# Where VectorE sums a small gate network inside a matmul kernel: part of it one unit earlier, the rest one operation a slot

## The chip, the cores and the metric

One core of a Trainium2 chip runs the whole program. The metric is the device time of one execution in microseconds (us). The kernel before takes 2253.77 us (median of three runs, 2252.57 to 2255.48). Engines are named as in the profile: PE (TensorE), DVE (VectorE), ACT (ScalarE), POOL (GpSimd), SP (the queue from which nearly all DMAs are issued).

## The reference, cut to what matters

`x` is 2 x 2048 x 512, fp32. Layer 0 puts each batch row `b` through three experts (hidden width 2048): two shared ones and one that a label selects. A gate per row, made from token 0 alone, weighs them. Layer 1 multiplies by a selected 512 x 512 matrix. Both layers are residual.

```
eo, s0, s1 = dense(x, wi[label], wo[label]), dense(x, swi[0], swo[0]), dense(x, swi[1], swo[1])
gate_in = concat([eo[:, 0], s0[:, 0], s1[:, 0]])             # 1536 numbers per row
w = softmax(relu(gate_in @ g1) @ g2)                         # g1: 1536 x 512, g2: 512 x 3
x = x + eo * w[0] + s0 * w[1] + s1 * w[2]
x = x + x @ W[cat] + b[cat]
```

## The kernel before, in words

The rows are cut into four blocks of 1024 tokens. The work is a list of twelve **units** (`units`, L109): units 0 to 3 are shared expert 0 on the four blocks, 4 to 7 shared expert 1, 8 and 9 the selected expert of row 0, 10 and 11 that of row 1. A unit is an up-projection (`up`, L743) and a down-projection (`down`, L882), each done by a two-level fast matrix product with 7 x 7 small products.

**Slots.** The order of everything is written out by hand. `up` has 7 stages (`i` in the order 1, 6, 2, 5, 7, 4, 3), each of 14 slots (`SEQ_UP`, L410, numbered s = 0 to 13). A slot issues two 128 x 256 matmuls, and the profile keeps two records of each, so a slot is 4 records and a stage 56. `down` has 49 slots (`SLOTS_DN`), numbered 0 to 48 here, of 8 records each.

**Seeds.** The products of a stage add up in PSUM banks, and what is in a bank is read out between two products that go into it, plus an older partial sum ("seed" below). In `up`: at s = 0, 1 product x1 is read into the z bank (L815, or ACT L813 in the stages 1 and 5); at s = 4, 5 x6 is read (L821); at s = 7, 8 x7 is read and a second sum is made (L821, L826); at s = 10, 11 L839; at s = 12, 13 L845. The next product into the same bank can't start before the read is done: x6 (s = 4, 5) waits for the reads of s = 0, 1; x7 (s = 7, 8) for those of s = 4, 5. `wide` (L776) and `make_tops` (L715) add DVE sums of 1024 columns, three of them at s = 11, 12, 13 of stage `i` = 5 and one at s = 1 of the next. In `down` the same reads are L947, L955, L957, L964, L966, with operand sums L733 to L740 and L904 and the block sums `y_sums` (L910).

**Background work.** `other_bg` is a list of generators; `step(other_bg)` (L871, L1022), at the end of every slot, advances the first one to its next `yield`. DVE, PE, ACT and SP each take their instructions in the order in which this program emits them, so what a generator emits stands behind that slot's seeds and ahead of the next slot's.

- `gate(b, 8)` (L1037) is appended at the end of units 8 and 10 and so runs in the first stages of units 9 and 11. It loads all of `g1` (3 MB, L1042) and a broadcast `g2` (L1044), waits 8 slots, then emits twelve multiply-adds into `hid` one a slot (L1052, L1054), three slots later a matmul `pg` over the partitions (L1059), relu `act` (L1062), three products `prod` (L1066), one reduction over 1536 columns (L1069), and the softmax (L1071 to L1081).
- `layer1(blk, 14)` (L1126) stands behind it, and also runs in unit 10 for the block of unit 9. It starts with `layer1_weights` (L1087): load W and a bias row, wait 14 slots, add the identity to W's diagonal (four 128 x 128 sums in one slot, L1101), then a matmul `pb` (L1104) and a copy (L1105). Then come 8 row tiles, 7 slots each: scaling on ACT (L1146), sums on POOL (L1151), four 512-column matmuls `po` (L1114), the result (L1122).
- `premix(blk, 10)` (L1169) is appended at the start of unit 11's `down`, behind `layer1` of unit 10's block: five loads of `acc` and `pm`, `layer1_weights` with a wait of 10 slots, then sixteen multiply-adds one a slot (L1192). At slot 47 whatever is left is emitted at once; `last_mix` (L1199) and the last 64 `po` records follow.

Weight blocks `w` come through 12 buffers, each fetched on SP 12 uses ahead (`used_w`, L631). The pool `io` has two buffers of 128 x 512 (tag `xn`).

Of the kernel before, what the change touches and what calls it, by code (L numbers as in the profile page):

```python
# [8 lines left out]
F32 = mybir.dt.float32  # L9
AF = mybir.ActivationFunctionType  # L10
ALU = mybir.AluOpType
AX = mybir.AxisListType
# [3 lines left out]
P = 128  # L16
# [3 lines left out]
ADD, SUB = ALU.add, ALU.subtract  # L20
# [16 lines left out]
def cond_resid_kernel(  # L37
# [22 lines left out]
    nc = tc.nc  # L60
    B, S, D = x.shape
# [681 lines left out]
    def up(n, xg, tops, y):  # L743
# [12 lines left out]
        for j, i in enumerate(I_UP(n)):  # L756
            mode, dst, src = plan[i]
            store = mode == "store"
            if dst not in O:
                O[dst] = qtile(n, f"h{dst}")  # L760
            if i == 5:
                O[12] = qtile(n, "h12")
            if n == 0 and i == 1:
                O[21] = qtile(n, "h21")
            half = lambda q, cc, d: blk_of(O[q], cc)[:, 2 * d : 2 * d + 2, :]
            bank, sn, seed = {}, {}, {}

            def relu(q, cc):
                v = blk_of(O[q], cc)
                nc.scalar.activation(v, v, AF.Relu)  # L770

            def wide(q, cc):


                o = blk_of(O[q], cc)
                nc.vector.tensor_tensor(o, blk_of(O[22], cc), blk_of(O[21], cc), ADD)  # L776
                if q == 22:
                    relu(22, cc)

            wides = {  # L780
                5: {11: (12, 11), 12: (12, 22), 13: (12, 21)},
                7: {1: (12, 12), 11: (22, 11), 13: (22, 22)},
                4: {1: (22, 21), 11: (22, 12)},
            }.get(i, {})
            done = False
            if i == (5 if n else 3):
                tg = make_tops(n, O, 1, 11, tops, y)
            top_at = {5: (2, 5), 3: (1, 11)}.get(i, ()) if n else (1, 3, 11, 13)
            for s, (bk, k, d) in enumerate(SEQ_UP):
                first = (bk, k) in (("x", 1), ("y", 5))  # L790
                if first:
                    bank[bk, d] = ps.tile(
                        [P, 2, TQ], F32, tag=bk, name=f"u{bk}_{n}_{i}_{d}"
                    )
                p = bank[bk, d]
                wt = w_tiles[n, 0, i, k]
                for g in range(2):
                    nc.tensor.matmul(  # L798
                        p[:, g, :],
                        lhsT=wt[:, 2 * d + g, :],  # L800
                        rhs=x_ops[n, i, k],
                        start=first and g == 0,
                        stop=True,
                        skip_group_check=True,
                    )
                if all(kk != k for _, kk, _ in SEQ_UP[s + 1 :]):
                    used_w()
                if k == 1:
                    z = bank["z", d] = ps.tile(
                        [P, 2, TQ], F32, tag="z", name=f"uz_{n}_{i}_{d}"  # L810
                    )
                    if store:
                        nc.scalar.activation(z, p, AF.Copy)  # L813
                    else:
                        nc.vector.tensor_tensor(z, p, half(src, 11, d), ADD)  # L815
                elif bk == "x" and k in SNAP:
                    t = snp.tile([P, 2, TQ], F32, tag="sn", name=f"us_{n}_{i}_{k}_{d}")
                    if store:
                        nc.scalar.activation(t, p, AF.Copy)  # L819
                    else:  # L820
                        nc.vector.tensor_tensor(  # L821
                            t, p, half(src, 12 if k == 6 else 22, d), ADD
                        )
                    sn[SNAP[k], d] = t
                    if k == 7:
                        nc.vector.tensor_tensor(  # L826
                            half(dst, 22, d), bank["y", d], t, ADD
                        )
                        if d == 1 and i in final:
                            relu(dst, 22)  # L830
                elif bk == "z":
                    nc.scalar.activation(  # L832
                        half(dst, 11, d), p, AF.Relu if i in final else AF.Copy
                    )
                elif k == 4:
                    if store:
                        nc.scalar.activation(half(dst, 21, d), p, AF.Copy)
                    else:
                        nc.vector.tensor_tensor(  # L839
                            half(dst, 21, d), p, half(src, 21, d), ADD  # L840
                        )
                    if d == 1 and i in final:
                        relu(dst, 21)
                elif k == 3:
                    nc.vector.tensor_tensor(half(dst, 12, d), p, sn["b", d], ADD)  # L845
                    if d == 1 and i in final:
                        relu(dst, 12)
                if s in wides:
                    wide(*wides[s])
                if n == 0 and i == 2:  # L850

                    for cc in {1: (11, 22), 2: (21,), 3: (12,)}.get(s, ()):
                        nc.scalar.activation(blk_of(O[21], cc), blk_of(O[11], cc), AF.Copy)
                if n == 0:
                    begin.outer({(2, 2): (7,), (6, 2): (3,)}.get((i, s), ()))
                    if (i, s) == (2, 2):
                        begin.second()
                    elif i in (5, 7) and s in (2, 5, 8, 11):
                        next(begin.ahead, None)
                    elif (i, s) == (4, 1):  # L860
                        for _ in begin.ahead:
                            pass
                if xg and j < 6 and not done and (
                    s >= 7 if i in (7, 4) else s % 2 == 0 or j == 0
                ):
                    done = advance(xg, 1)
                if s in top_at:
                    next(tg, None)
                prep_paced(RATE_UP[j])
                if n or j or s >= 7:  # L870
                    step(other_bg)  # L871
                if s == 4 and n not in MAKES and j + 2 < NP:
                    fetch_parts(n, I_UP(n)[j + 2])
            if xg and j < 6 and not done:
                advance(xg)
            if n in MAKES:
                keep_parts(n, i)
# [4 lines left out]
    def down(n, H, tops, y, prepare):  # L882
# [124 lines left out]
        for s, (i, name) in enumerate(SLOTS_DN):  # L1007
# [11 lines left out]
            prepare(s)  # L1019
            prep_paced(0.0)  # L1020
            prep_run(RUN_DN.get((i, name), 0))
            step(other_bg)  # L1022
        for _ in job:
            pass
# [7 lines left out]
        nc.sync.dma_start(out=ys[slot_y, blk], in_=yf)  # L1032

    gin = [const.tile([P, NX, DC], F32, name=f"gin_{b}") for b in range(B)]
    gates = {}

    def gate(b, lag):  # L1037


        g1t = [bigp.tile([P, 4, D], F32, tag=t, bufs=1, name=f"g1{t}_{b}") for t in ("raw", "o", "t")]  # L1040
        for j in range(NX):
            nc.sync.dma_start(out=g1t[j], in_=g1_v[:, j * DC : (j + 1) * DC, :])  # L1042
        g2b = bigp.tile([P, D, NX], F32, tag="s", bufs=1, name=f"g2b_{b}")
        nc.sync.dma_start(out=g2b, in_=g2.rearrange("(o d) n -> o d n", o=1).to_broadcast([P, D, NX]))  # L1044
        for _ in range(lag):
            yield
        hid = small.tile([P, D], F32, tag="hid", name=f"hid_{b}")
        for k in range(NX * DC):
            j, c = divmod(k, DC)
            col = gin[b][:, j, c : c + 1]  # L1050
            if k == 0:
                nc.vector.tensor_scalar(hid, g1t[j][:, c, :], col, None, ALU.mult)  # L1052
            else:
                nc.vector.scalar_tensor_tensor(hid, g1t[j][:, c, :], col, hid, ALU.mult, ADD)  # L1054
            yield
        for _ in range(3):
            yield
# [4 lines left out]
        nc.scalar.activation(act, pg, AF.Relu)  # L1062
        yield
        prod = bigp.tile([P, NX, D], F32, tag="o", bufs=1, name=f"prod_{b}")
        for j in range(NX):
            nc.vector.tensor_tensor(prod[:, j, :], act, g2b[:, :, j], ALU.mult)  # L1066
            yield
        logit = small.tile([P, NX], F32, tag="logit", name=f"logit_{b}")
        nc.vector.tensor_reduce(logit, prod, AX.X, ALU.add)  # L1069
        mx = small.tile([P, 1], F32, tag="mx", name=f"mx_{b}")  # L1070
        nc.vector.tensor_reduce(mx, logit, AX.X, ALU.max)  # L1071
        nc.vector.tensor_scalar(logit, logit, mx, None, ALU.subtract)
# [14 lines left out]
    def layer1_weights(blk, lag, also=None):  # L1087
# [7 lines left out]
        for k in range(lag):  # L1095
            yield
            if k == 5 and also:
                also()
        for c in range(DC):
            v = w1[:, c, c * P : (c + 1) * P]  # L1100
            nc.vector.tensor_tensor(v, v, ident, ADD)  # L1101
        yield
        pb = ps.tile([P, D], F32, tag="m", name=f"pb_{blk}")
        nc.tensor.matmul(pb, lhsT=ones[0:1, :], rhs=brow, start=True, stop=True)  # L1104
        nc.vector.tensor_copy(bias, pb)  # L1105
# [117 lines left out]
    with tc.manual_schedule():  # L1223
# [18 lines left out]
        for n, (e, blk) in enumerate(units):  # L1242
            if n == 0:
                for e0, k0 in [(e0, k0) for e0 in range(1, NE) for k0 in range(2)]:
                    preps[e0, k0] = Prep(e0, k0)
            tops = {}
            if n:
                y = yp.tile([P, DC, 4, TQ], F32, tag="y", name=f"y_{n}")
            H = up(n, xg, tops, y)
# [81 lines left out]
```

## Time and profile before

| | |
|---|---|
| three timed runs | 2252.57, 2253.77, 2255.48 us |
| the profiled execution, its own time | 2255.11 us |
| its span in the profile | 2253.3 us |
| granted TensorE clock in it | 0.994 |
| busy: PE / DVE / ACT / POOL | 2195.0 / 1637.5 / 544.4 / 722.4 us |
| HBM traffic | 421.80 MB read, 157.81 MB written |

How to read it: times in the views count from the start of the span, which is 1.8 us shorter than the execution's time. "Idle before" names what an engine waited for; only waits of an engine whose work ends last cost time. Units 8 to 11 begin near 1433, 1603, 1810 and 2010 us.

### The profile page before, as it was taken

To read this page: it belongs to the slowest core of one execution; us is meant where nothing else is said; L and a number is where in the kernel's file an instruction comes from. 1 tells how busy PE (TensorE), PEld (TensorE's weight loads), DVE (VectorE), ACT (ScalarE), POOL (GpSimd) and SP (SyncE) were. 2 spreads that over 40 slices of the span, in tenths; PEclk is the share of its full clock that TensorE was granted. 3 is DMA by queue.
4 is the path that set the end of the run, shared out by engine and by line. 5 is a ranking of instruction groups with operands and counts; after the bars stand their busy time and mean duration, and the time that the engine had idled before them with its cause. 6 is when DMAs were issued, how large, how long until landed. Compare 5 with 4: busy or idle time off the path is not lost.

```text
span 2253.3 us, 28548 instructions
## 1 busy us (share of the span) xinstructions
PE 2195.0 (97%) x9808; PEld 1851.5 (82%) x9808; DVE 1637.5 (73%) x2028; ACT 544.4 (24%) x937; POOL 722.4 (32%) x580
## 2 busy tenths in 40 slices
PE   8999998999999999999999999999999999999999
PEld 6787887888888888888888888888877877887786
DVE  7897778587688587587587587587676846767695
ACT  3221230331231231231131141131133133113310
POOL 5787522560850430340350340330033023002300
PEclk9999999999999999999999999999999999999999
DMA  9853996897997896896997896896896697579671
GB/s 339 317 170 108 352 311 210 292 312 253 301 327 217 289 326 179 301 310 205 300 311 216 273 333 215 274 335 183 294 293 185 185 318 227 153 250 321 207 276 56
DMA packets 484059, 581.55 MB, mean 258 GB/s; under 512 B 28360, under 2 KB 316104, under 8 KB 480716
## 3 DMA queue, kind: packets, MB, share of 16 engines
q1 hardware_dynamic: 480188, 572.90, 78.3%
q10 hardware_dynamic: 3728, 6.82, 0.9%
q8 instruction: 80, 1.31, 0.2%
q14 instruction: 63, 0.52, 0.1%
HBM read 421.80 MB, written 157.81 MB: 257 GB/s over the span
## 4 chain that ended last, share of the span: by engine, by line
PE 80%; DVE 9%; DMA 2%; POOL 2%; issue 1%; SPq 0%; ACT 0%; DVEq 0%; POOLq 0%; ACTq 0%
PE dx L933 23%; PE ux L798 20%; PE dy L933 12%; PE uy L798 9%; PE dz L933 6%; PE po L1114 5%; PE uz L798 5%; DVE h L904 1%; DMA w<-ws_s 1%; DVE h L776 1%; DMA g1raw<-in_L_cond_g_dram 1%; DVE y L910 1%; DVE hid L1054 1%; DVE us L821 1%; DVE h L845 1%
## 5 line engine op out<-in xcount | busy, mean ns | idle before, releaser
L798 PE MATMUL ux<-xs,w 128*128 128x256 f32 x1792 | 429.8, 381 | 11.0 <-DVE sm L1077 3.1
L933 PE MATMUL dx<-t,w 128*128 128x256 f32 x1680 | 399.2, 381 | 13.8 <-DVE ds L955 13.8
L798 PEld LDWEIGHTS ux<-xs,w 128*128 128x128 f32 x1792 | 337.5, 190 | 73.9 <-DVE us L821 9.6
L933 PEld LDWEIGHTS dx<-t,w 128*128 128x128 f32 x1680 | 319.2, 191 | 59.2 <-DVE ds L955 13.7
L1151 POOL TENSOR_TENSOR mix<-mix 128x512 f32<-128x512 f32 x72 | 102.3, 1421 | 523.9 <-DMA w<-ws_t 316.5
L821 DVE TENSOR_TENSOR us<-ux,h 128x512 f32<-128x512 f32 x240 | 162.7, 686 | 117.6 <-PE ux L798 117.2
L904 DVE TENSOR_TENSOR h<-h,h 128x1024 f32<-128x1024 f32 x192 | 241.1, 1271 | 0.0
L770 ACT ACTIVATE h<-h 128x1024 f32<-128x1024 f32 x156 | 164.5, 1056 | 240.2 <-DVE h L826 111.8
L798 PE MATMUL uy<-xs,w 128*128 128x256 f32 x896 | 214.4, 380 | 4.1 <-DVE h L845 3.9
L826 DVE TENSOR_TENSOR h<-uy,us 128x512 f32<-128x512 f32 x168 | 116.1, 692 | 112.3 <-ACT us L819 107.8
L798 PEld LDWEIGHTS uy<-xs,w 128*128 128x128 f32 x896 | 169.4, 190 | 34.3 <-DVE h L845 7.5
L832 ACT ACTIVATE h<-uz 128x512 f32<-128x512 f32 x168 | 99.5, 592 | 377.3 <-PE uz L798 350.5
L933 PE MATMUL dy<-h,w 128*128 128x256 f32 x672 | 160.4, 382 | 4.8 <-DVE y L957 4.8
L681 POOL TENSOR_TENSOR seen<-pulse 1x1 f32<-1x1 f32 x18 | 11.8, 656 | 474.7 <-DVE pulse L680 474.7
L798 PE MATMUL ux<-xi,w 128*128 128x256 f32 x640 | 154.1, 384 | 7.9 <-DVE us L821 2.8
L141 POOL TENSOR_TENSOR po<-pr 128x384 f32<-128x384 f32 x48 | 51.6, 1090 | 332.0 <-DMA w<-ws_s 127.4
L776 DVE TENSOR_TENSOR h<-h,h 128x1024 f32<-128x1024 f32 x96 | 146.1, 1522 | 7.0 <-ACT h L832 5.6
L845 DVE TENSOR_TENSOR h<-uy,us 128x512 f32<-128x512 f32 x168 | 113.0, 687 | 52.3 <-PE uy L798 50.1
L933 PEld LDWEIGHTS dy<-h,w 128*128 128x128 f32 x672 | 128.0, 191 | 23.8 <-issue 5.2
L933 PE MATMUL dz<-h,w 128*128 128x256 f32 x616 | 145.6, 379 | 0.1
L933 PE MATMUL dx<-h,w 128*128 128x256 f32 x616 | 145.5, 379 | 0.0
L798 PEld LDWEIGHTS ux<-xi,w 128*128 128x128 f32 x640 | 121.1, 191 | 29.7 <-issue 11.8
(155 smaller groups left out, 3332.7 us busy)
## 6 DMA issues: line engine op xcount, KB each, us to landing
w<-ws_t SPq DMA_DIRECT2D x352, 256.0 KB, 4.1
w<-ws_s SPq DMA_DIRECT2D x270, 256.0 KB, 4.3
w<-ws_o SPq DMA_DIRECT2D x264, 256.0 KB, 4.8
xs<-xs SPq DMA_DIRECT2D x56, 896.0 KB, 6.9
ws_s<-ps SPq DMA_DIRECT2D x24, 1024.0 KB, 7.6
ws_t<-pt SPq DMA_DIRECT2D x24, 1024.0 KB, 5.8
ys<-y SPq DMA_DIRECT2D x11, 2048.0 KB, 8.3
ws_o<-po SPq DMA_DIRECT2D x24, 768.0 KB, 7.6
```

Of the source, the lines that this page charges most:

```text
L141: eng.tensor_tensor(o, i0, i1, op)
L770: nc.scalar.activation(v, v, AF.Relu)
L776: nc.vector.tensor_tensor(o, blk_of(O[22], cc), blk_of(O[21], cc), ADD)
L798: nc.tensor.matmul(p[:, g, :], lhsT=wt[:, 2 * d + g, :], rhs=x_ops[n, i, k], start=first and g == 0, stop=True, skip_group_check=True,)
L821: nc.vector.tensor_tensor(t, p, half(src, 12 if k == 6 else 22, d), ADD)
L826: nc.vector.tensor_tensor(half(dst, 22, d), bank["y", d], t, ADD)
L832: nc.scalar.activation(half(dst, 11, d), p, AF.Relu if i in final else AF.Copy)
L845: nc.vector.tensor_tensor(half(dst, 12, d), p, sn["b", d], ADD)
L904: nc.vector.tensor_tensor(bl(o), bl(i0), bl(i1), SUB)
L933: nc.tensor.matmul(p, lhsT=wt[:, g, :], rhs=op[g], start=first and g == 0, stop=True, skip_group_check=True,)
L1114: nc.tensor.matmul(po[t], lhsT=mixed[c], rhs=l1[blk][0][:, c, :], start=(c == 0), stop=(c == DC - 1),)
L1151: nc.gpsimd.tensor_tensor(m[:, 3, :, :], m[:, 3, :, :], m[:, j, :, :], ADD)
```

## The change

`gate_shared(b)` is new. It is appended at the start of units 8 and 10 (`n in (2 * NB, 2 * NB + NBB)`), loads the eight 128 x 512 pieces of `g1` that belong to the shared experts one by one into the `xn` buffers, and emits the eight multiply-adds for them, five slots or more apart. `gate` keeps four multiply-adds and one load of 1 MB. A flag `quiet` is set in `up` at s = 0 to 3 and 11 to 13 and throughout `down`; `when_quiet` yields until it is set. The eight operations, the four that are left, the products, the reduction (cut into three of 512 columns) and the four diagonal sums each wait for such a slot and have one to themselves.

```
@@ up @@
             for s, (bk, k, d) in enumerate(SEQ_UP):
+                quiet[0] = s in (0, 1, 2, 3, 11, 12, 13)
@@ down @@
+            quiet[0] = True
             step(other_bg)
@@ new @@
+    def when_quiet():
+        while not quiet[0]:
+            yield
+    def gate_shared(b):
+        hid = hids[b] = small.tile([P, D], F32, tag="hid", name=f"hid_{b}")
+        t = {}
+        def fetch(k):
+            t[k] = iop.tile([P, D], F32, tag="xn", name=f"g1_{b}_{k}")
+            nc.sync.dma_start(out=t[k], in_=g1_v[:, k, :])
+        fetch(DC)
+        for k in range(DC, NX * DC):
+            if k + 1 < NX * DC:
+                fetch(k + 1)
+            for _ in range(4):
+                yield
+            yield from when_quiet()
+            j, c = divmod(k, DC)
+            col = gin[b][:, j, c : c + 1]
+            if k == DC:
+                nc.vector.tensor_scalar(hid, t[k], col, None, ALU.mult)
+            else:
+                nc.vector.scalar_tensor_tensor(hid, t[k], col, hid, ALU.mult, ADD)
+            yield
@@ gate @@
-        g1t = [bigp.tile([P, 4, D], F32, tag=t, bufs=1, name=f"g1{t}_{b}") for t in ("raw", "o", "t")]
-        for j in range(NX):
-            nc.sync.dma_start(out=g1t[j], in_=g1_v[:, j * DC : (j + 1) * DC, :])
+        g1t = bigp.tile([P, DC, D], F32, tag="raw", bufs=1, name=f"g1_{b}")
+        nc.sync.dma_start(out=g1t, in_=g1_v[:, :DC, :])
...
-        for k in range(NX * DC):
...
+        hid = hids[b]
+        for c in range(DC):
+            yield from when_quiet()
+            col = gin[b][:, 0, c : c + 1]
+            nc.vector.scalar_tensor_tensor(hid, g1t[:, c, :], col, hid, ALU.mult, ADD)
             yield
...
         for j in range(NX):
+            yield from when_quiet()
             nc.vector.tensor_tensor(prod[:, j, :], act, g2b[:, :, j], ALU.mult)
             yield
-        nc.vector.tensor_reduce(logit, prod, AX.X, ALU.add)
+            yield from when_quiet()
+            nc.vector.tensor_reduce(logit[:, j : j + 1], prod[:, j : j + 1, :], AX.X, ALU.add)
+            yield
@@ layer1_weights @@
         for c in range(DC):
+            yield from when_quiet()
             v = w1[:, c, c * P : (c + 1) * P]
             nc.vector.tensor_tensor(v, v, ident, ADD)
-        yield
+            yield
@@ main loop @@
+            if n in (2 * NB, 2 * NB + NBB):
+                other_bg.append((f"s{n}", gate_shared((n - 2 * NB) // NBB)))
```

More of the change, by code (lines that the diff above doesn't have):

```diff
@@ L1034, in cond_resid_kernel @@
     gin = [const.tile([P, NX, DC], F32, name=f"gin_{b}") for b in range(B)]
-    gates = {}
+    gates, hids = {}, {}
+    quiet = [True]
+    def when_quiet():
[21 more added lines that the diff above has]
+            yield
     def gate(b, lag):
-        g1t = [bigp.tile([P, 4, D], F32, tag=t, bufs=1, name=f"g1{t}_{b}") for t in ("raw", "o", "t")]
-        for j in range(NX):
-            nc.sync.dma_start(out=g1t[j], in_=g1_v[:, j * DC : (j + 1) * DC, :])
+        g1t = bigp.tile([P, DC, D], F32, tag="raw", bufs=1, name=f"g1_{b}")
+        nc.sync.dma_start(out=g1t, in_=g1_v[:, :DC, :])
         g2b = bigp.tile([P, D, NX], F32, tag="s", bufs=1, name=f"g2b_{b}")
@@ L1046, in gate @@
             yield
-        hid = small.tile([P, D], F32, tag="hid", name=f"hid_{b}")
-        for k in range(NX * DC):
[L1049 to L1054, printed above, removed]
+        hid = hids[b]
[3 more added lines that the diff above has]
+            nc.vector.scalar_tensor_tensor(hid, g1t[:, c, :], col, hid, ALU.mult, ADD)
             yield
@@ L1064, in gate @@
         prod = bigp.tile([P, NX, D], F32, tag="o", bufs=1, name=f"prod_{b}")
+        logit = small.tile([P, NX], F32, tag="logit", name=f"logit_{b}")
         for j in range(NX):
+            yield from when_quiet()
             nc.vector.tensor_tensor(prod[:, j, :], act, g2b[:, :, j], ALU.mult)
             yield
-        logit = small.tile([P, NX], F32, tag="logit", name=f"logit_{b}")
-        nc.vector.tensor_reduce(logit, prod, AX.X, ALU.add)
+            yield from when_quiet()
+            nc.vector.tensor_reduce(logit[:, j : j + 1], prod[:, j : j + 1, :], AX.X, ALU.add)
+            yield
         mx = small.tile([P, 1], F32, tag="mx", name=f"mx_{b}")
```

## The prediction, written before the changed kernel was run

> **What bounds the kernel now.** First the page: the busy times, then the chain that ended last.
>
> ```profile
> PE 2195.0 (97%) x9808; PEld 1851.5 (82%) x9808; DVE 1637.5 (73%) x2028; ACT 544.4 (24%) x937; POOL 722.4 (32%) x580
> ...
> PE 80%; DVE 9%; DMA 2%; POOL 2%; issue 1%; SPq 0%; ACT 0%; DVEq 0%; POOLq 0%; ACTq 0%
> ```
>
> PE sets the time, and the change takes no matmul away. It can only win back time in which PE stands still, so I looked for where that is. I took the distance between the first matmuls of successive stages in the timeline and subtracted the records in between, at 0.215 us for 256 columns and 0.429 us for 512 (a 56-record stage without a stall then takes 12.04 us). What is left, "loss", is 0.05 us for most stages. Up-projection of unit 8: 1.18 us in all. Unit 9: 0.05, 4.04, 1.94, 1.12, 0.43, 0.43, 0.43, together 8.45. Unit 10: 3.10. Unit 11: 0.05, 4.18, 1.95, 1.12 and three times 0.43, together 8.59, and its down-projection 4.26 (0.44, 1.36 and 2.28 in its third to fifth stages). 4 and 2 us stand exactly where the gate runs. The 0.43 are the price of two `po` tiles.
>
> Next, busy time by stretch: the two gates, and the same 25 us of unit 8.
>
> ```profile
> core 0: us, PE busy (x) PEld busy (x) DVE busy (x) ACT busy (x) POOL busy (x), PEclk, DMA share, GB/s
> 1615.00:1640.00 25.00, 21.03 (x88) 15.77 (x88) 23.64 (x39) 2.00 (x4) 0.00 (x0) 1.00 0.99 365
> 2022.00:2047.00 25.00, 20.89 (x88) 15.65 (x87) 23.69 (x39) 2.00 (x4) 0.00 (x0) 1.00 0.98 367
> 1445.00:1470.00 25.00, 25.00 (x117) 22.03 (x116) 16.93 (x25) 4.19 (x6) 13.89 (x12) 1.00 1.00 317
> ```
>
> In the gate DVE is full (23.6 of 25) and PE is not; in unit 8 it is the other way round. Then DVE's timeline in the first gate:
>
> ```profile
> 1615.12 0.49 DVE L1052 TENSOR_SCALAR hid<-g1raw,gin 128x512 f32<-128x512 f32 x1 [2.21 <-DMA g1raw<-in_L_cond_g_dram]
> 1615.64 2.33 DVE L1054 SCALAR_TENSOR_TENSOR hid<-g1raw,gin,hid 128x512 f32<-128x512 f32 x3
> 1617.88 0.68 DVE L845 TENSOR_TENSOR h<-uy,us 128x512 f32<-128x512 f32 x1
> 1618.48 0.74 DVE L1054 SCALAR_TENSOR_TENSOR hid<-g1o,gin,hid 128x512 f32<-128x512 f32 x1
> ...
> 1631.79 0.85 DVE L1066 TENSOR_TENSOR prod<-act,g2b 128x512 f32<-128x512 f32 x1
> ...
> 1635.90 1.74 DVE L1069 TENSOR_REDUCE logit<-prod 128x3 f32<-128x1536 f32 x1
> ```
>
> Every slot of 0.86 us holds a seed (next start 0.60 later) and a gate operation (0.66): 1.26 us of DVE. PE waits for the seeds (waits of PE's weight loads, 1613 to 1640):
>
> ```profile
> PEld ux L798 <- DVE sm L1077: 2.0, 1, 2.0
> PEld uy L798 <- DVE h L845: 2.0, 2, 1.4
> PEld ux L798 <- DVE us L821: 1.8, 2, 1.2
> PEld ux L798 <- DVE uz L815: 1.3, 3, 0.5
> ```
>
> "sm" is only what stood last in DVE's queue: the seed behind it was late because of the 1.74 us reduction.
>
> **The gate in units 9 and 11.** Eight of twelve multiply-adds leave. I followed slots against DVE's queue. With a wait of 8 slots, three of the four land at s = 11, 12, 13 of stage 1 and one at s = 0 of stage 2, beside the L845 seeds (0.60 each) and the z seeds. DVE work from s = 12 on: seed, 0.78, seed, 0.78, seed, 0.78, seed; the seed of s = 0 is read 3.4 us after the first, and x6 needs it 4.05 us after: no stall, and the seed of s = 1 fits too (4.7 against 4.9). `g1raw` landed 10.4 us after its issue with 2 MB more behind it; if the 1 MB takes as long, everything shifts by 0.85 us and stalls up to 0.8. I take 0.3. Stage 2 then costs 0.30 for the `pg` records plus 0.05 plus 0.3 = 0.65 instead of 4.04.
>
> The products and reductions fall on s = 11 to 13 of stage 2 and 0 to 2 of stage 3. A 512-column reduction is not in the trace. Two rows give it: 3 columns 0.156 us (L1071), 1536 columns 1.750, so 0.153 + 512 x 1.04 ns = 0.69, bounds 0.58 (a third) and 1.75. Queue: 0.60 + 0.77, 0.60 + 0.73, 0.60 + 0.77, 0.60 + 0.73, 0.60 + 0.77, 0.73, then the small ones (0.5): the z seed of s = 1 is done 0.2 us after x6 wants its bank, and the x6 seeds of s = 4, 5 start 1.5 us late, 0.7 to 0.9 us more than x7 allows, then 0.4. Stage 3: 1.7 instead of 1.94. Here the stall only changes its name.
>
> The cutting itself adds 2 x 0.15 = 0.3 us of DVE per gate, which is within that 1.7. [...]
>
> **W's diagonal.** Four sums of 0.284 us (start to start 0.22). Before, they came at s = 2 of stage 4, where ACT does the z seeds and DVE idles. With the later gate and `quiet` they come 12 slots later in all: s = 11, 12, 13 of stage 4 (`i` = 5, where three `wide` sums stand) and s = 0 of stage 5, then `pb` and its copy (0.60). In unit 8 the seeds of stage 5 are already a touch late there (0.39 loss). They get 0.45 and 0.66 us later; the two `pb` records (1.15 us on PE) come just before x6 and give that time back. Then the copy delays the x6 seeds and x7 waits 0.6. Stage 5: 0.3 (`pb`) + 0.6 + 0.2 = 1.1 instead of 0.43; stage 4: 0.05 instead of 1.12, since `pb`, `po` and mixing have left it. Stages 6 and 7: 0.43 each. Three `po` tiles move into the down-projection, whose slots are 1.72 us and whose loss is 0.05 with DVE at about 80%: nothing, at most 0.4.
>
> Unit 9: 0.05 + 0.65 + 1.7 + 0.05 + 1.1 + 0.86 = 4.4 instead of 8.45: **-4.05**. Unit 11: 4.4 instead of 8.59: **-4.2**. Bounds of each: -6.7 if stages 2, 3 and 5 lose nothing but their own records, -1 if stages 3 and 5 lose 2.5 us more.
>
> **Unit 8 gets eight multiply-adds** (0.75 us each, two a stage: s = 11 and 2), until s = 2 of stage 5. In stages 1 to 4 they meet idle DVE (16.93 of 25 above). The last stands behind the stage-5 `wide`, where DVE is 10.96 of 12 busy, and moves the x6 seeds by 0.7, which x7 feels in full. **+0.8**; bounds 0 (all hidden) and 8 x 0.75 = 6. POOL works in this unit and not in the gate. `wide` (L776) takes 1.21 to 2.35 us over the run, which I put down to POOL; 0.75 may then become 1.4 for some, which the upper bound holds. [...]
>
> SP gets eight 256 KB loads, and each waits for the multiply-add two before. Behind them stand the fetches of w. These land in 7.3 us in this stretch (median 4.1 over the run) and are issued 12 uses, about 20 us, ahead: 12 us of cover against waits of 1 to 2 us. If that cover went, PE would lose those waits, up to 8 x 1 us. A load is issued 12 us before its multiply-add, so DVE shouldn't wait; behind such a wait stand seeds, and PE waits for them.
>
> **Unit 10:** its multiply-adds fall into two up-stages and then slots 2 to 22 of the down-projection, with one every five slots of 1.72 us: 0, at most +1. Its diagonal goes from one slot to s = 0 to 3: the 0.76 us that PE waited behind it may go, but `po` moves by three slots: 0, bounds -0.8 and +0.8.
>
> **The last down-projection.** This is the part that the diff doesn't show. `layer1` ends 12 slots later in unit 11, so `premix` starts at slot 16 instead of 4, its diagonal at 26 to 29 instead of 14, its sixteen multiply-adds at 31 to 46 instead of 16 to 31. Before, DVE was full where they stood (busy time by stretch), and PE waited (timeline of PE and DVE):
>
> ```profile
> 2163.00:2197.00 34.00, 31.52 (x143) 26.48 (x142) 33.90 (x43) 3.81 (x10) 0.00 (x0) 1.00 0.65 219
> ```
>
> ```profile
> 2161.84 0.90 DVE L1101 TENSOR_TENSOR w<-w,ident 128x128 f32<-128x128 f32 x4 [1.71 <-DMA w<-in_L_cond_W_dram]
> ...
> 2182.96 1.99 PE L933 MATMUL dy<-h,w 128*128 128x256 f32 x8 [0.74 <-DVE y L957]
> ...
> 2191.94 1.99 PE L933 MATMUL dx<-t,w 128*128 128x256 f32 x8 [1.39 <-DVE ds L955]
> ```
>
> That loss (4.26 in all) goes, another comes. Counted from the start of slot 29, with start-to-start times 1.13 (L904, L733), 0.66 (L1192), 1.33 (a pair of L910) and 0.34 to 0.46 (seeds), DVE is never idle from slot 32 on: at slot 35 its work ends at 17.0 us while PE is at 13.2, at slot 38 at 26.3 against 18.4. `y` of slot 39 (L957) is done at 26.7, and y3 of slot 42, ready at 24.4, waits 2.4 us for it. ACT waits for `y_sums` at slot 36 and makes x7 0.8 late. After slot 42 DVE catches up, and the last `po` finds its operands. Loss 2.4 + 0.8 + 0.3 (`pb`) + 0.4 (others) = 3.9: **-0.4**. W landed 20.2 us after `premix` began; again so, it lands at the start of slot 29, and DVE has just enough to do after that. Each us later is one us more at slot 42. Bounds -3 (no stall) and +3.
>
> **Sum** against the profiled execution (span 2253.3, own time 2255.11): -4.05 - 4.2 + 0.8 + 0 - 0.4 = -7.8, so 2247.3. The median of the runs is 1.34 below that execution, which gives **2246.0**.
>
> **Rivals.**
> 1. *The gate's stall moves instead of going*: the z seeds of stage 3 and the crowd at `i` = 5 lose 2.5 us more in each gate. For it: DVE has 1.3 us per slot there still. Against: stage 2 (4 us) is relieved in any case. -7.8 + 5 = -2.8: 2251.
> 2. *Unit 8 pays it back*: all eight multiply-adds show, 6 instead of 0.8. For: DMA share 1.00 and POOL busy. Against: 8 us of idle DVE per 25. -2.6: 2251.
> 3. *The gate costs only its records*: -6.7, -6.85, +0.8, -0.4 = -13.1: 2240.7.
> 4. *Slower*: in the last down-projection W lands late, and `premix` stands wholly in the last 20 slots. The price is a us per us; with more than 7.8 us (W after 28 us instead of 20) the kernel is slower, and with 13 it takes 2259. For: 6 MB are loaded in one piece, ahead of it. Against: the same loads took 20.2 us at 367 GB/s, and nothing is added to them.
> 5. *It doesn't do what it says*: no; in the changed program's order on each engine the operations stand in the slots named above.
>
> **Chances.** Forecast 0.60 (2242.5 to 2249), rivals 1 and 2 0.15 and 0.07 (near 2251), 3 0.12, 4 0.06. A measurement of this kernel can tell about 0.2% (4.5 us) from no change: below 2249.3 is faster, 0.60 + 0.12; rivals 1 and 2 are the same, 0.22; slower 0.06. The range 2240 to 2252 leaves out rival 4 and the ends of 3 and 2, about 0.15.
>
> **What would show it.** Stage losses by the same count: unit 9 and 11 stage 2 under 1 us (right) or over 2 (wrong); stage 3 near 1.7; stage 5 near 1.1; unit 8's stage 5 near 1.1; a wait of "dy" for L957 of 2 to 3 us late in the last down-projection. A DVE wait of more than 1 us for W there, or for `g` tiles in unit 8, would make it wrong, as would a PE wait for w.

## The result, and the profile after

| | us |
|---|---|
| after, median of seven runs | 2263.89 (2260.02 to 2270.04) |
| before, median of seven runs beside them | 2253.77 (2252.57 to 2257.02) |
| ratio, 95% interval | 1.0045 [1.0035, 1.0056] |
| after's profiled execution, own time / span | 2269.35 / 2267.6 |

The forecast was 2246.0, 0.35% faster; the kernel is 0.45% slower. The page of after, its line of busy times and the engines of the chain that ended last:

```profile
PE 2196.7 (97%) x9808; PEld 1854.9 (82%) x9808; DVE 1651.3 (73%) x2032; ACT 544.5 (24%) x937; POOL 728.7 (32%) x580
...
PE 79%; DVE 8%; DMA 3%; POOL 3%; issue 1%; SPq 1%; ACT 0%; DVEq 0%; POOLq 0%; ACTq 0%
```

PE's work is the same, so again only the losses tell. Counted as in the prediction, in us (the last two columns are kernels described below; "sum" is over these units):

| | before | predicted | after | e1_act_queue | v2_shared_in_down |
|---|---|---|---|---|---|
| unit 8, up | 1.18 | 2.0 | **13.88** | 3.88 | 1.37 |
| unit 9, up | 8.45 | 4.4 | 4.43 | 4.81 | 3.60 |
| unit 9, down | 0.33 | 0.3 to 0.7 | **2.33** | 2.32 | 0.33 |
| unit 10, up | 3.10 | 3.1 | 0.73 | 0.73 | 0.73 |
| unit 11, up | 8.59 | 4.4 | 4.43 | 4.42 | 3.60 |
| unit 11, down | 4.26 | 3.9 | **9.82** | 9.82 | 3.68 |
| sum | 25.9 | 18.1 | 35.6 | 26.0 | 13.3 |

After minus before is 9.7 us, and the medians differ by 10.1: units 8 to 11 hold the whole result. In units 0 to 7, where nothing was changed, this one execution happens to be 4.4 us longer.

The gate's sum came out as forecast, though by errors that cancel (below). Busy time by stretch of after, some 11 us into units 9 and 11 as before, and the same 25 us of unit 8:

```profile
core 0: us, PE busy (x) PEld busy (x) DVE busy (x) ACT busy (x) POOL busy (x), PEclk, DMA share, GB/s
1449.00:1474.00 25.00, 22.81 (x106) 19.78 (x105) 17.35 (x25) 1.89 (x4) 12.75 (x11) 1.00 0.98 322
1495.00:1502.00 7.00, 5.39 (x12) 3.60 (x13) 6.84 (x8) 0.00 (x0) 6.92 (x5) 0.52 0.99 342
1632.00:1657.00 25.00, 24.48 (x110) 20.29 (x109) 22.04 (x38) 2.96 (x6) 0.00 (x0) 1.00 0.93 341
2035.00:2060.00 25.00, 24.47 (x110) 20.29 (x109) 22.02 (x38) 3.31 (x6) 0.00 (x0) 1.00 0.92 335
```

PE is busy 24.5 of 25 us in the gates instead of 21. But unit 8 has lost 2.2 us in the first row, and the second row has a granted clock of 0.52. What happened there is read from three engines. SP's queue, DVE and PE around 1480 to 1502 us of after:

```profile
1480.86 9.74 SPq L179 DMA_DIRECT2D pr<-in_L_cond_wo_dram  x8
1490.70 0.38 SPq L1052 DMA_DIRECT2D g<-in_L_cond_g_dram  x1
```

```profile
1486.23 1.22 DVE L776 TENSOR_TENSOR h<-h,h 128x1024 f32<-128x1024 f32 x1 [0.23 <-ACT h L833]
1495.16 0.79 DVE L1066 SCALAR_TENSOR_TENSOR hid<-g,gin,hid 128x512 f32<-128x512 f32 x1 [7.70 <-DMA g<-in_L_cond_g_dram]
1495.87 0.68 DVE L846 TENSOR_TENSOR h<-uy,us 128x512 f32<-128x512 f32 x1
```

```profile
1496.61 4.01 PE L799 MATMUL uy<-xs,w 128*128 128x256 f32 x8 [5.92 <-DVE h L846]
1500.48 2.76 PE L799 MATMUL ux<-xs,w 128*128 128x256 f32 x8
1503.08 1.03 PE L799 MATMUL uz<-xs,w 128*128 128x256 f32 x4
```

Eight loads of `pr` (raw weights for the background sums on POOL, L179) take SP 9.7 us to issue. One piece of `g1` stands behind them. DVE waits 7.7 us for it, a seed (L846) stands behind the multiply-add, and PE waits 5.9 us for the seed. Then PE's next records take 0.48 us each instead of 0.215: the granted clock is halved from 1495.2 to 1502.1. Part of that falls into the pause; the twelve records from 1496.61 on take 5.6 us instead of 2.6, so the half clock costs another 3.0 us. The same block of `pr` stood in before, and there unit 8 lost 1.18 us: nothing that DVE waits for in order stood behind it. (Before, SP's queue:)

```profile
1472.68 9.84 SPq L179 DMA_DIRECT2D pr<-in_L_cond_wo_dram  x8
```

### The profile page after: what moved, and what is told of

The parts are those of the page before. It is cut to its first block, busy times and chain, and to the rows that moved or that the text cites. A ratio compares the mean times of both kernels' runs of the same rounds, so it can differ in the third digit from the quotient of the medians.

```text
span 2267.6 us, 28578 instructions
## 1 busy us (share of the span) xinstructions
PE 2196.7 (97%) x9808; PEld 1854.9 (82%) x9808; DVE 1651.3 (73%) x2032; ACT 544.5 (24%) x937; POOL 728.7 (32%) x580
## 4 chain that ended last, share of the span: by engine, by line
PE 79%; DVE 8%; DMA 3%; POOL 3%; issue 1%; SPq 1%; ACT 0%; DVEq 0%; POOLq 0%; ACTq 0%
PE dx L934 22%; PE ux L799 20%; PE dy L934 11%; PE uy L799 9%; PE dz L934 6%; PE uz L799 5%; PE po L1146 5%; DVE h L776 1%; DMA w<-ws_s 1%; DVE h L905 1%; DVE y L911 1%; POOL ps L141 1%; SPq L179 1%; POOL po L141 1%; DVE h L846 1%
## 5 line engine op out<-in xcount | busy, mean ns | idle before, releaser
L1183 POOL TENSOR_TENSOR mix<-mix 128x512 f32<-128x512 f32 x72 | 107.8, 1497 | 536.9 <-ACT mix L1178 527.0
L827 DVE TENSOR_TENSOR h<-uy,us 128x512 f32<-128x512 f32 x168 | 116.2, 691 | 114.4 <-ACT us L820 110.1
L681 POOL TENSOR_TENSOR seen<-pulse 1x1 f32<-1x1 f32 x18 | 10.9, 605 | 475.9 <-DVE pulse L680 475.9
L776 DVE TENSOR_TENSOR h<-h,h 128x1024 f32<-128x1024 f32 x96 | 147.0, 1531 | 4.2 <-ACT h L833 2.9
L934 PE MATMUL dy<-t,w 128*128 128x256 f32 x576 | 136.2, 379 | 0.0
```

The lines of the kernel that those rows point to most:

```text
L827: nc.vector.tensor_tensor(half(dst, 22, d), bank["y", d], t, ADD)
L934: nc.tensor.matmul(p, lhsT=wt[:, g, :], rhs=op[g], start=first and g == 0, stop=True, skip_group_check=True,)
L1183: nc.gpsimd.tensor_tensor(m[:, 3, :, :], m[:, 3, :, :], m[:, j, :, :], ADD)
```

## The experiments

All are built on after. "Time" is the median, with the ratio to the runs of before on the same chip and its 95% interval. The theory was: order on SP and DVE's fixed order make unit 8; layer1 and premix standing later make the two down-projections.

**e1_act_queue.** Line 1052:

```
-            nc.sync.dma_start(out=t[k], in_=g1_v[:, k, :])
+            nc.scalar.dma_start(out=t[k], in_=g1_v[:, k, :])
```

> The eight loads of gate_shared are issued from ACT's queue, everything else is as after. Theory (order on SP): in unit 8 the loads stood on SP behind eight prep loads that took 9.8 us to issue, DVE waited 7.7 us for one of them with seeds behind it, and PE stood for the seeds; from ACT's queue the load goes out when it is emitted, so unit 8's up-projection loses 1 to 3 us instead of 13.9, DVE's wait for g in it is under 1 us, and the time is 9 to 12 us less than after's (2252 to 2255). Rival (the eight operations contend with POOL for SBUF): nothing moves, loss 12 to 14 us, time as after's. Rival (bandwidth, 2 MB more in a stretch with a DMA share of 1.00): nothing moves either, or PE waits for w. The other losses (9, 10, 11) stay within 1 us of after's under each of them; ACT may pass on up to 1 us where a load has to wait for its buffer.

Time 2254.74, ratio 1.000 [0.999, 1.001]. DVE's waits for `g` in unit 8, after and then e1 (in all, times, longest):

```profile
DVE hid L1066 <- DMA g<-in_L_cond_g_dram: 12.2, 4, 7.7
```

```profile
DVE hid L1064 <- DMA g<-in_L_cond_g_dram: 0.5, 1, 0.5
```

Unit 8 loses 3.88, the other units are as in after. One queue was worth the 9 to 10 us. What is left is a little over the bound: waits for `w` of 2.2 us that before didn't have.

**e2_one_load** and **e3_loads_only** part the eight operations from the eight loads.

```
e2:
-            if k + 1 < NX * DC:
-                fetch(k + 1)
+            t[k] = t[DC]
e3:
-            else:
-                nc.vector.scalar_tensor_tensor(hid, t[k], col, hid, ALU.mult, ADD)
```

> Only the first of the eight pieces of g1 is loaded, and all eight operations of gate_shared read it, in the same slots as in after (the gate's sum is therefore another one). Theory (order on SP): unit 8's up-projection loses 1 to 3 us instead of 13.9, since nothing but the first operation can wait for a load; time 2252 to 2255. Rival (operations and POOL): the loss stays at 12 to 14 us, since all eight operations are there. Rival (bandwidth): the loss goes, as by the theory; the next kernel parts those two.

> All eight loads of gate_shared stay where they are on SP, but only its first multiply-add is made; the other seven are left out (the gate's sum is another one). Theory (order on SP, DVE waiting in order): unit 8's up-projection loses 1 to 2.5 us, as in before, though the loads are as late as in after; time 2251 to 2255. Rival (bandwidth): the loss stays at 12 to 14 us and PE or DVE waits for w or pr instead. Rival (operations and POOL): the loss goes, as by the theory; the kernel with one load parts those two.

e2: 2255.39, 1.0002 [0.9992, 1.0011], unit 8 loses 2.29. e3: 2258.12, 1.0012 [1.0002, 1.0021], unit 8 loses 5.67, twice the upper end of what the theory allowed: 2.15 us are one wait for `w`, and about 1.6 more the half clock that follows it (granted from 1495.2 to 1498.6). PE's waits (weight loads left out) in unit 8's up-projection, after, then e2, then e3:

```profile
PE uy L799 <- DVE h L846: 8.1, 2, 5.9
...
PE ux L799 <- DVE us L822: 1.5, 1, 1.5
```

```profile
PE ux L799 <- DVE us L822: 0.9, 1, 0.9
...
PE ux L799 <- DVE uz L816: 0.2, 1, 0.2
```

```profile
PE ux L799 <- DMA w<-ws_t: 2.2, 1, 2.2
...
PE ux L799 <- DVE uz L816: 0.3, 1, 0.3
```

So the big wait needs both, a late load and an operation on DVE that waits for it. The operations alone cost 1.1 us here (2.29 - 1.18; forecast 0.8), but that isn't clear of the spread: without any of them the same up-projection lost 1.18 (before), 1.26 (e4), 1.37 and 2.82 us (the two v2 below). The loads have a price without the operations too, `w` is late by 2.2 us. Whether that is bandwidth, as the rival had it, isn't shown: in e1 SP waits 1.1 us for a `g` load to land before it issues a `pr` load, so the new loads also hold up issues (see e7). In the eight kernels whose eight loads go out in that up-projection without holding DVE up (e1, e3, e5 to e8, e10, e12), PE's waits for `w` in it add up to 2.2 to 3.8 us; in before, e2 and both v2 there are none.

**e4_quiet_only** leaves `gate_shared` out and lets the gate make all twelve multiply-adds in quiet slots; **e5_shared_alone** keeps it (loads on ACT's queue) and removes every `when_quiet` from the gate and the diagonal (`gate_shared` keeps its own), with one whole reduction.

```
e4 (gate):
+        for k in range(NX * DC):
+            yield from when_quiet()
e5 (gate, layer1_weights):
-            yield from when_quiet()
```

> No gate_shared: the gate loads all of g1 as before and makes its twelve multiply-adds, products, cut reductions and the diagonal one a quiet slot. Unit 8 is then as in before: loss 1.2 us by the theory. For the gate: twelve operations on seven quiet slots a stage take 24 slots, so the products come a stage later; each operation stands beside a seed that is not read for some slots. If the quiet slots are what helps, the gate's units lose 4 to 5.5 us each instead of 8.5 (stage 1 and 2 under 1 each); if it is the fewer operations, they lose 7 us or more. layer1 ends some 25 slots later than in before, so the last down-projection loses 6 to 12 us by what after's trace shows (9.8), against 4.3 if its loss doesn't depend on where premix stands. Sum: 2250 to 2260, unclear against before.

> gate_shared with its loads on ACT's queue as in e1, and the rest of the gate as in before: four multiply-adds, three products and one whole reduction one after the other without regard to the slot, the four diagonal sums in one slot. Theory (what is won in the gate is the eight operations; what is lost behind it comes from layer1 and premix standing 12 slots later): layer1 now ends 8 slots earlier than in before, so the down-projection of unit 9 loses 0.3 as in before and the last one 2.5 to 4.5, instead of 2.3 and 9.8 in e1; the up-projections of units 9 and 11 lose 5 to 6.5 each (the reduction and the diagonal still stall) against 4.4 to 4.8 in e1. Time 5 to 8 us less than e1's (2247 to 2250). Rival (the spreading is what helps the gate, and premix's place doesn't matter): units 9 and 11 lose 7 to 8.5, the last down-projection 8 to 10, time 2257 to 2261.

e4: 2257.93, 1.0014 [1.0005, 1.0024]; units 9 and 11 up lose 4.26 and 4.10. e5: 2256.33, 1.0003 [0.9993, 1.0012]; they lose 8.13 and 6.13, the down-projections 0.33 and 4.04. e5 was a miss (losses of 5 to 6.5 us and a time of 2247 to 2250 were expected). One operation a quiet slot, with the cut reduction and the spread diagonal, gives all of the gate's gain as a sum, and fewer operations alone a small, uneven part (0.3 and 2.5 us). That part is clouded by a late load: in e5 DVE takes up the four multiply-adds at s = 8 and then waits 3.0 us for the gate's piece of `g1`, with seeds behind it; in after three of the four stand at s = 11 or later. But twelve operations in quiet slots push layer1 so far back that in e4 premix isn't done at slot 47, and PE waits for it before the last 64 records (e4, PE's timeline):

```profile
2210.95 1.89 PE L934 MATMUL dy<-h,w 128*128 128x256 f32 x8
2221.61 30.69 PE L1151 MATMUL po<-w,acc 128*128 128x512 f32 x64 [8.77 <-DVE acc L1241]
```

So the eight operations made one unit ahead do not free the gate; they keep what follows the gate in time.

**e6_early_layer1** is e1 with layer1 brought forward.

```
 gate:
-        g2b = bigp.tile([P, D, NX], F32, tag="s", bufs=1, name=f"g2b_{b}")
+        g2b = bigp.tile([P, D, NX], F32, tag="t", bufs=1, name=f"g2b_{b}")
+        loaded[b * NBB] = load_weights(b * NBB)
-        act = bigp.tile([P, D], F32, tag="raw", bufs=1, name=f"act_{b}")
+        act = iop.tile([P, D], F32, tag="xn", name=f"act_{b}")
 units:
-                    other_bg.append((f"l{blk}", layer1(blk, 14)))
+                    other_bg.append((f"l{blk}", layer1(blk, 14 if blk % NBB else 4)))
```

> e1 with layer1 brought forward by 10 slots in units 9 and 11: W and the bias row are loaded with the gate's loads, g2 lies in another buffer for it, act in one of the xn buffers, and layer1 waits 4 slots instead of 14. Everything in the gate's slots is as in e1. Theory (place of layer1 and premix): up-projections of 9 and 11 as in e1 within 1 us (4.4 to 4.8), down-projection of unit 9 0.3 to 0.6 instead of 2.3, the last one 4 to 6 instead of 9.8; time 6 to 8 us less than e1's (2247 to 2249). Rival (the last down-projection loses its 9.8 because DVE has too much work there wherever premix stands): last one 8 to 10, time within 2.5 us of e1's.

2248.81, 0.9967 [0.9956, 0.9978]. Units 9 and 11 up 3.6 each, down 0.33 and 3.61. The theory holds: place, not amount of work. (W's load and layer1 moved together; e6 doesn't part the two.)

**e7_premix_act** moves the loads of `acc` and `pm` to ACT's queue (`nc.sync` to `nc.scalar` in L1207 and L1216).

> e1 with premix's loads of acc and pm (5 MB) issued from ACT's queue instead of SP; W and the bias row stay on SP. Theory (order on SP, as in unit 8): W and the weight blocks w no longer stand behind these loads, so the 2.1 us that PE waits for w in the fourth stage of the last down-projection go, and DVE's wait for W (2.9 us in after) goes; the 3.3 us in the sixth stage shrink by at most 1. Time 2 to 3 us less than e1's. Rival (bandwidth: the 6 MB are in flight at once whatever queue issues them): fourth stage stays at 2 to 2.8 us, DVE still waits 2 to 4 us for W, time as e1's within 1.5 us.

2265.16, 1.0041 [1.0027, 1.0055], 9 us over before and 10 over e1, which neither side expected. ACT's timeline, then PE's:

```profile
2161.37 10.33 ACTq L1216 DMA_DIRECT2D pm<-ys  x3
2171.74 0.38 ACT L954 ACTIVATE ds<-dx 128x256 f32<-128x256 f32 x1 [10.92 <-issue]
```

```profile
2163.69 1.89 PE L934 MATMUL dx<-h,w 128*128 128x256 f32 x8
2172.18 3.78 PE L934 MATMUL dx<-t,w 128*128 128x256 f32 x8 [6.59 <-ACT ds L954]
```

ACT was not held by `pm`'s buffers, which are layer1's last `mix` buffers: POOL's last sum in them ends at 2143.57, and the last `po` record that reads them starts at 2154.63. The first `pm` load goes out at 2161.37. The second waits until 2170.43 for semaphore 104, and the trace has the landing of this load of SP's on that semaphore at 2170.41:

```profile
2162.02 0.57 SPq L474 DMA_DIRECT2D w<-ws_t  x1
```

The DMAs of this program report their landing on eight semaphores in turn (100, 102, 104, 105 and 107 to 110; in after 1765 DMAs of SP's queue and 25 of ACT's share them, and a `pr` load waits 1.0 us on SP for the landing of the `ys` write ahead of it on 104), and here a load on ACT's queue waited for the one before it on its semaphore. With it waited what stood behind it on ACT, a seed: ACT was held for 10.9 us and PE for 6.6. So here the second queue didn't part its loads from those on SP. The fourth stage's wait for `w` did go (PE has none there), as the theory had it, but the kernel can't settle what SP's order alone is worth there, since 10 us of ACT moved with it.

**e8_later2** was meant to move layer1 by two slots (`layer1(blk, 14 if blk % NBB else 16)`).

> e1 with layer1 two slots later in units 9 and 11 (a wait of 16 slots instead of 14). The three scalings on ACT that stood just ahead of dz at the first slots of the down-projections of 9 and 11 then stand two slots further on. Theory (the 2.05 us in the first stage of both come from that one meeting on ACT): they fall to under 0.6 in both units, or to the price of another meeting under 1.2; premix is two slots later too, and the last down-projection loses 1 to 3 us more in its fifth to seventh stages. Sum: -3 and +2, time as e1's within 2 us. Rival (they come from the change of projection itself with DVE late, not from the scalings): 2.05 stays in both units.

2255.62, 1.0004 [0.9994, 1.0013]; 2.05 stays in both units. It tells nothing about the theory: the diagonal had been waiting for s = 11 in any case, the two slots vanished in that wait, and the order on every engine is e1's. It serves as a second profile of e1: unit 8 loses 4.24 (3.88 there), the last down-projection 7.57 (9.82 there). So much, 2 us, one stretch can differ between two executions of the same work.

**e10_layer1_plus2** puts the two slots behind the diagonal.

```
         l1[blk] = (w1, bias)
-        yield
+        for _ in range(1 if blk % NBB else 3):
+            yield
```

> e1 with two more slots between layer1's bias copy and its first row tile in units 9 and 11 (e8's two slots were taken up by the wait for a quiet slot and changed no order). The three scalings on ACT that stood just ahead of dz at the start of the down-projections now stand two slots on. Theory (the 2.05 us there come from that one meeting): first stage of the down-projections of 9 and 11 under 0.6 us, or under 1.2 if another relu or dz is met; the last down-projection as in e1 and e8 (7.6 to 9.8, less the 1.5 to 2) or up to 2 us more for premix two slots later. Time 1 to 4 us less than e1's. Rival (DVE's lateness at the change of projection): 2.05 stays in both.

2252.58, 0.9982 [0.9972, 0.9992]. ACT at the start of unit 11's down-projection in after, and of unit 9's in e10:

```profile
2133.06 1.06 ACT L770 ACTIVATE h<-h 128x1024 f32<-128x1024 f32 x1 [1.87 <-DVE h L846]
2134.03 1.93 ACT L1178 ACTIVATE mix<-mix,g 128x512 f32<-128x512 f32 x3
2135.86 0.36 ACT L946 ACTIVATE dz<-dx 128x256 f32<-128x256 f32 x1
```

```profile
1721.70 1.06 ACT L770 ACTIVATE h<-h 128x1024 f32<-128x1024 f32 x1 [2.03 <-DVE h L846]
1722.76 0.37 ACT L946 ACTIVATE dz<-dx 128x256 f32<-128x256 f32 x1
1723.04 1.94 ACT L1179 ACTIVATE mix<-mix,g 128x512 f32<-128x512 f32 x3
```

The scalings now follow dz, and the first stage loses 0.05 and 0.06 instead of 2.05. The rival is out.

**v2_shared_in_down** is e6 with `gate_shared` of row 0 appended ahead of unit 8's `down` instead of its `up`; **v2_loads_on_sp** is v2 with L1052 as in after.

```
-                other_bg.append((f"s{n}", gate_shared((n - 2 * NB) // NBB)))
             ...
+                other_bg.append((f"s{n}", gate_shared((n - 2 * NB) // NBB)))
             down(n, H, tops, y, prepare)
```

> e6 with gate_shared of row 0 in unit 8's down-projection instead of its up-projection (in unit 10 it stood there already). Theory: the eight operations cost something in the up-projection because the stages 3, 5 and 6 of unit 8 have no idle DVE where they fall; the down-projection's slots are 1.72 us and its loss was 0.3 to 0.55 in unit 10 with the same operations. Unit 8: up-projection 1.0 to 1.6 us instead of 3.9 to 5.0, down-projection 0.3 to 0.6; units 9 to 11 as in e6 (3.6, 0.3, 0.7, 0.6, 3.6, 3.6). Time 3 to 4 us less than e6's: 2244 to 2247. Rival (the operations cost the same beside any stage with prep sums on POOL): the loss comes back in the down-projection, time as e6's.

> v2 with gate_shared's loads issued from SP again, as in after. Theory (only the prep loads ahead of them on SP made them late; unit 8's down-projection has none): nothing moves, unit 8's down-projection 0.3 to 0.6, time as v2's within 1.5 us. Rival (SP is a bad place for these loads anywhere in unit 8, or w behind them comes late): DVE waits for g by more than 1 us there, the loss rises to 3 us or more.

v2: 2244.67, 0.9955 [0.9938, 0.9973]; on SP: 2245.25, 0.9948 [0.993, 0.9966]. Both beat both kernels. SP is no bad place for these loads; behind the `pr` block it is. Unit 8's up-projection, the same work in both, lost 1.37 us and 2.82 us.

**e12_no_pool_mix0** asks why the fifth stage lost 2.90 where 1.1 was forecast.

```
-                nc.gpsimd.tensor_tensor(m[:, 3, :, :], m[:, 3, :, :], m[:, j, :, :], ADD)
+                if t or blk % NBB:
+                    nc.gpsimd.tensor_tensor(m[:, 3, :, :], m[:, 3, :, :], m[:, j, :, :], ADD)
```

> e1, but POOL's three sums for the first row tile of layer1 in units 9 and 11 are left out (that tile's output is another one); every other instruction and every slot is as in e1. In after and e1 the fifth stage of units 9 and 11 lost 2.90 us where 1.1 was predicted; wide sums of 1.21 us took 2.17 and 1.75 there and a diagonal sum of 0.28 took 1.35, while POOL made these three sums. Theory (VectorE sums with both inputs in SBUF are slowed by POOL's sums): wide back to 1.2, the diagonal sums to 0.28, fifth stage 0.9 to 1.4 us in both units. Rival (the queue of wide, diagonal and seeds is as long without POOL): fifth stage stays at 2.5 to 2.9 us. The time by one look: 2 to 4 us under e1's by the theory.

The stage loses 0.44 in both units (one run: 2250.14, with before at 2255.76 beside it). DVE in unit 9, after and then e12:

```profile
1671.10 2.17 DVE L776 TENSOR_TENSOR h<-h,h 128x1024 f32<-128x1024 f32 x1
1673.19 1.35 DVE L1133 TENSOR_TENSOR w<-w,ident 128x128 f32<-128x128 f32 x1
1674.46 0.68 DVE L846 TENSOR_TENSOR h<-uy,us 128x512 f32<-128x512 f32 x1
1675.06 1.75 DVE L776 TENSOR_TENSOR h<-h,h 128x1024 f32<-128x1024 f32 x1
```

```profile
1658.24 1.22 DVE L776 TENSOR_TENSOR h<-h,h 128x1024 f32<-128x1024 f32 x1
1659.38 0.28 DVE L1133 TENSOR_TENSOR w<-w,ident 128x128 f32<-128x128 f32 x1
1659.58 0.68 DVE L846 TENSOR_TENSOR h<-uy,us 128x512 f32<-128x512 f32 x1
1660.18 1.22 DVE L776 TENSOR_TENSOR h<-h,h 128x1024 f32<-128x1024 f32 x1
```

In after POOL makes three `mix` sums from 1670.91 to 1675.73. The DVE sums of two SBUF tiles took 2.17, 1.35 and 1.75 us there, and 1.22, 0.28 and 1.22 without POOL's sums; the seed L846, with one input in PSUM, took 0.68 in both. The forecast of the queue's length was too long by itself: 0.44, not 1.1.

## Why the prediction was wrong, by its steps

- **The step that failed: "A load is issued 12 us before its multiply-add, so DVE shouldn't wait".** I took the emission for the issue, and asked of SP only what stands behind the new loads, not what stands ahead of them. The 9.84 us of `pr` were in before's trace. e1 shows the price: unit 8 loses 10.0 us less, of +12.7. With this step right (a late load, seeds behind it) the forecast's -7.8 would have turned to about +2 by itself. The prediction named the sign, a DVE wait of more than 1 us for `g` in unit 8; it was 12.2.
- **Unit 8's eight operations, +0.8:** e2 has +1.1, which agrees but is no more than what this stretch varies by without them (1.18 to 2.82). The upper bound of 6, all operations on the path, held no wait for a load, so the +12.7 lies outside it. The cover of `w`, left as "if that cover went", did go in part: 2.2 to 3.8 us (e1 and its kind).
- **The gate, -4.05 and -4.2:** measured -4.0 and -4.2, but that is luck, errors cancel. Stage 2 loses 0.05, not 0.65; stage 3 1.29, not 1.7; stages 6 and 7 0.05 each, not 0.43; stage 5 2.90, not 1.1, of which POOL's sums make 2.46 (e12). The 0.43 are not the price of two `po` tiles either: after has the same tiles in these stages without it, and in e10, two slots on, it is back. The cause named first was wrong too: not that eight operations leave, but that what is left stands in quiet slots (e4 against e5). The reduction of 512 columns, estimated 0.69, takes 0.675.
- **"Three `po` tiles move into the down-projection ... nothing, at most 0.4":** +2.0 in unit 9, and the same in unit 11. I weighed PE and DVE for the tiles and forgot ACT, whose three scalings fell just ahead of dz (e10). That ACT is busy 24% of the span says nothing about one slot.
- **The last down-projection, -0.4:** measured +5.6. Right: W landed 19.9 us after premix began (20.2 assumed), and PE waited 2.12 us for L958 (2.4) and 0.62 for ds (0.8). Not in the sum: the 2.05 above, 2.0 us for a `w` that stood on SP behind premix's loads, and a half clock after the 2.12 us pause (3.61 us for eight records, 1.7 too long). e6 shows that the place of premix makes it: 3.61.
- **Unit 10, 0 with bounds +-0.8:** measured -2.4. With the diagonal in quiet slots, stalls of 1.18, 0.79 and 0.94 in three stages shrank to 0.44, 0.05 and 0.05 (e5, without them, keeps 1.04, 0.79 and 0.93); I had counted only 0.76 behind one.
- **Rival 4** was on the right side with a wrong mechanism, W instead of `g`. Rival 2 had the right unit, with the operations' time in place of the load's wait.

PE's lines at the end of after's last down-projection, for the fifth point:

```profile
2195.44 1.96 PE L934 MATMUL dz<-h,w 128*128 128x256 f32 x8 [1.97 <-DMA w<-ws_s]
...
2214.81 1.99 PE L934 MATMUL dx<-t,w 128*128 128x256 f32 x8 [0.62 <-ACT ds L954]
...
2222.38 3.61 PE L934 MATMUL dy<-h,w 128*128 128x256 f32 x8 [2.12 <-DVE y L958]
```

## What to carry to other kernels

For every load that a change adds, list what is ahead of it on its queue as well as behind it, and for every operation that waits for it, what is behind that on its engine: here the same block of `pr`, 9.8 us on SP, went with a loss of 1.18 us in unit 8 in before and of 13.88 in after, where DVE waited for a load behind it, with seeds in line. When background work gets longer, follow what comes after it to the end of the program, on every engine; here that was worth nearly as much (e6 against e1, 6 us) as all that the change won in the gate (8.2 us). And before you credit a gain to work that leaves, ask whether moving it alone would give the same.

## What the runs showed of the hardware

- **Half clock after short pauses.** After PE's pauses of 5.9 us or more the next matmuls ran at half clock each time: 5.99 and 6.35 (after and before, near 22 us), 5.92 (after, granted 0.52 from 1495 to 1502), 6.59 (e7, 0.58 from 2171 to 2177), 8.77 (e4, 0.50 from 2221 to 2226) and 10.94 in unit 1 of before and of after (0.5 from 391 to 402 and from 389 to 403). A pause of 2.1 us did it sometimes: the same wait of 2.1 us for L958 was followed by half clock in after and e7 (eight records in 3.61 and 3.43 us) and by full clock in e1 and e2 (1.99). In after a stall of 2.1 us thus cost 3.8 (2.1 and the 1.7 above). When the clock changed can be read from the profiles of before and after: in each, all changes of the granted clock (9 and 11) lie whole multiples of 3.4133 us apart, to 0.02 us. On that grid, each of the eight full-clock steps in which PE stood still for 2.0 us or more (three in before, five in after, up to 2235 us) was followed by half clock; of the twelve with 1.5 to 1.95 us, one was (1.67 us, in before). Of after's pause of 2.12 us, 2.02 lay in one step. So here a step needn't be idle throughout; what makes the clock change is not shown.
- **`wide` on DVE beside POOL.** Over after's whole run, `wide` (L776, both inputs in SBUF) takes at most 1.23 us where POOL is idle (33 of them) and 1.74 in the median, up to 2.34, where POOL is busy for most of it (53). Seeds with a PSUM input (L846) have a median of 0.68 with and without POOL. The prediction left room for this in unit 8's upper bound; it decided the fifth stage instead (2.90 us against 0.44 in e12).
- **What stood ahead on a queue.** Eight loads of 128 KB took SP 9.7 us in after, 5.55 of them the first load and about 0.6 each of the others; whether the 5.55 are initiating or a wait that the profile doesn't name, no run tells. Moving `g` from behind them made e1 10 us faster than after, with the same 2 MB loaded, so here it counted what the queue held back. e7 shows the same from the other side: a load of ACT's queue waited for the landing of another, 8.4 us after that one's issue, and held ACT.
